# Sampling with source tiles of 9 by 14 for 3 by 8 positions, and hats of tile columns loaded into the weights' place

## Chip, cores, metric

One core of a Trainium2 chip. The metric is the device time of one execution in microseconds (us), the median of several; the fast runs of one kernel agree within 0.7% here, mostly within 0.4%, and all runs here were of the fast state. Engines: PE (TensorE, matmul), PEld (its weight loads), DVE (VectorE), ACT (ScalarE), POOL (GpSimd), SP (SyncE, which here only issues DMA).

## The reference, cut to what matters

Two layers on x of shape (2, 256, 128, 128). The first has three branches with dilations 1, 9 and 12. Each computes 18 offsets per pixel by a 3x3 convolution, samples x bilinearly at nine shifted places, weights the nine samples per channel and sums them.

```python
def _bilinear(x, py, px):            # four corners, each with weight (1-|py-yc|) * (1-|px-xc|)
    ...
def _deform_dw(x, offset, w, pad, dil):
    py = yy[None, None] - pad + ky[None, :, None, None] * dil + off[:, :, 0]
    px = xx[None, None] - pad + kx[None, :, None, None] * dil + off[:, :, 1]
    sampled = _bilinear(x, py, px)
    return jnp.einsum('bckhw,ck->bchw', sampled, wk)
# ... layer norm, gelu, sum of branches, 1x1 convolution, MLP, layer norm; then a ternary 3x3 convolution
```

The kernel turns sampling into matmuls. A tile of source pixels (8 rows by 16 columns, 128, with their channels) is the stationary operand. The moving operand A holds for each source pixel and each sampled position its bilinear weight: a *row hat*, max(0, 1-|dy|), times a *column hat*. Hats are computed first and kept in HBM; a unit of work (image, row block, branch) loads them for its tile rows and columns.

## The kernel before

The parts that the change touches, with `# ...` at cuts:

```python
RI, CI = 2, 10                                  # positions of a tile: 2 rows by 10 columns
TR, TC = RI + 2 * REACH, CI + 2 * REACH         # source pixels of a tile: 8 by 16 = 128 partitions

def load_hats(u):                               # issued on SP, a unit ahead
    for ky in taps(u):
        hy = pool.tile([P, RI, 3, W], F32, name="hy", tag="hy", bufs=3)
        hx = pool.tile([P, RI, 3, W], F32, name="hx", tag="hx", bufs=3)
        for h, first, dims in ((hy, 0, [[0, TC], [pitch, TR]]), (hx, TR, [[pitch, TC], [0, TR]])):
            nc.sync.dma_start(h[:, i0:i1]..., bass.AP(hq[first, y0]..., dims + [[1, (i1 - i0) * 3 * W]]))

def build(u, ky):                               # DVE: A = hy * hx, each tap shifted by its dilation
    pin(nc.vector.tensor_tensor(dst, hy[...], hx[...], ALU.mult))

def sample(u, c):                               # c: half of the channels
    tail.advance()                              # a slice of norm, gelu, MLP of rows that are done
    for T in range(0, NT, 2):
        # ... two matmuls of one source tile each (L759), then one copy PSUM -> ev (L768)
    if c == KC - 1:
        prepare(u + 2)                          # the products of unit u+2, then load_hats(u+3)
    for ky in kys:
        accumulate(u, c, ev, ky)                # DVE: ring += weight * ev, nine taps (L733)
```

`ev` holds sampled values, `ring` the rows of sums of a branch, and the tail is what is done with finished rows: norm, gelu, 1x1 convolution, MLP. The tail's own loads (`other`, `xn`, `xr`) are also issued on SP.

## Time and profile before

| | before |
|---|---|
| time | 7899 us (7881 to 7907) |
| first norm, offsets, hats | 0 to 981 us |
| sampling and tail | 981 to 6670 us |
| second convolution | 6670 to 7903 us |

The prediction below shows the lines that carry this. Only the sampling stage matters. Its slices of granted PE clock and DMA share, in tenths, over 40 equal parts of the span of the kernel before:

```profile
PEclk9999889999999999999999999999999999799999
DMA  8767799999999999998689999999999995222121
```

The clock is at nine tenths or more nearly throughout, and the DMA engines are 90% busy or more in nearly all of the stage.

### The profile page before, as it was taken

What the parts mean: (1) busy time and instruction counts of PE and PEld (TensorE: products, weight loads), DVE (VectorE), ACT (ScalarE), POOL (GpSimd) and SP (SyncE); (2) the same over time, 40 slices, a digit from 0 to 9 for tenths busy, and PEclk for the clock granted to TensorE, in tenths of its full rate; (3) what the DMA queues carried; (4) which work ended last, traced back from release to release, by engine and by line L of the source; (5) the groups of instructions that cost most, each with busy time, mean ns of one, the idle gap of its engine ahead of it and who ended that gap; (6) DMA issues with size and microseconds to landing.
All of it is one profiled execution on the core that took longest, in us unless ns stands there. A gap on an engine that the chain in (4) does not pass through costs nothing. (4 is left out here: it accounts for less than half of the span.)

```text
span 7903.1 us, 115440 instructions
## 1 busy us (share of the span) xinstructions
PE 7101.1 (90%) x37984; PEld 5421.9 (69%) x37984; DVE 6400.1 (81%) x13680; ACT 4514.7 (57%) x9350; POOL 715.1 (9%) x1292
## 2 busy tenths in 40 slices
PE   5999887899999999899988989999998999699999
PEld 2555577777887777777777777877787777344444
DVE  6666578888999889988688898898889986577776
ACT  1344355666666666667655666666666666333232
POOL 0000000111111111111100111111111111000000
PEclk9999889999999999999999999999999999799999
DMA  8767799999999999998689999999999995222121
GB/s 280 215 187 195 187 229 243 235 247 246 244 240 249 242 243 241 246 243 224 192 233 243 239 248 245 243 240 245 249 240 244 243 242 162 74 74 78 63 82 48
DMA packets 1011327, 1652.66 MB, mean 209 GB/s; under 512 B 120800, under 2 KB 573200, under 8 KB 1006360
## 3 DMA queue, kind: packets, MB, share of 16 engines
q1 hardware_dynamic: 993304, 1611.57, 76.3%
q10 hardware_dynamic: 17408, 33.56, 1.3%
q8 instruction: 304, 4.98, 0.3%
q14 instruction: 311, 2.55, 0.1%
HBM read 1376.69 MB, written 268.09 MB: 208 GB/s over the span
## 5 line engine op out<-in xcount | busy, mean ns | idle before, releaser
L759 PE MATMUL pm<-A,xs 128*128 128x180 f32 (+2 forms) x22288 | 3638.8, 319 | 578.6 <-ACT ev L768 551.2
L759 PEld LDWEIGHTS pm<-A,xs 128*128 128x128 f32 x22288 | 3431.7, 196 | 791.6 <-ACT ev L768 652.0
L768 ACT COPY ev<-pm 128x360 f32<-128x360 f32 (+2 forms) x5572 | 2283.3, 456 | 1517.3 <-DVE ring L733 751.3
L733 DVE SCALAR_TENSOR_TENSOR ring<-ev,defw,ring 128x256 f32<-128x256 f32 (+5 forms) x6272 | 2786.9, 463 | 212.5 <-ACT ev L768 43.2
L689 DVE TENSOR_TENSOR A<-hy,hx 128x768 f32<-128x768 f32 x1130 | 1018.7, 946 | 343.5 <-DMA hx<-hats 170.7
L487 ACT ACTIVATE T<-T,rs 128x256 f32<-128x256 f32 x1280 | 663.8, 595 | 3.3 <-POOL rs L483 3.2
L1083 PE MATMUL pc<-cring,signs 128*128 128x512 bf16 x2304 | 522.8, 386 | 56.1 <-DVE signs L971 23.6
L480 POOL TENSOR_SCALAR rs<-mv 128x4 f32<-128x4 f32 x320 | 108.0, 337 | 5108.0 <-DVE mv L478 4133.9
L1083 PE MATMUL pc<-cring,sums 128*128 128x512 bf16 x2304 | 510.3, 380 | 0.0
L446 PE MATMUL hp<-T,w 128*128 128x512 f32 x1024 | 490.7, 604 | 7.8 <-ACT T L565 7.8
L476 DVE BATCH_NORM_STATS2 st<-T 128x6 f32<-128x256 f32 x1280 | 446.9, 412 | 23.2 <-ACT T L468 23.2
L203 PE MATMUL pz<-wz,xa 128*128 128x486 f32 x1024 | 461.2, 584 | 4.3 <-DVE zr L210 4.3
L1083 PEld LDWEIGHTS <-signs 128*128 128x128 bf16 x2304 | 227.5, 99 | 340.7 <-issue 46.2
L446 PE MATMUL h<-hT,w 128*128 128x512 f32 x1024 | 460.1, 592 | 0.0
L1083 PEld LDWEIGHTS <-sums 128*128 128x128 bf16 x2304 | 225.4, 98 | 274.4 <-DVE sums L1143 0.2
L499 PEld LDWEIGHTS zc<-ident,T 128*128 128x128 f32 x2560 | 342.0, 156 | 98.2 <-issue 61.5
L515 ACT ACTIVATE T<-zc,bb,bw 128x512 f32<-128x512 f32 x384 | 278.5, 779 | 227.8 <-PE zc L499 226.8
L499 PE MATMUL zc<-ident,T 128*128 128x128 f32 x2560 | 384.5, 297 | 19.6 <-ACT T L487 14.1
L1067 ACT CAST cring<-D 128x2048 bf16<-128x2048 f32 x128 | 243.3, 1902 | 222.9 <-PE pc L1083 152.2
L482 POOL TENSOR_TENSOR rs<-rs,mhalf 128x4 f32<-128x4 f32 x320 | 369.6, 1155 | 0.0
L468 ACT COPY T<-tp 128x512 f32<-128x512 f32 x640 | 345.2, 599 | 38.0 <-PE tp L466 37.3
L1091 ACT ACTIVATE o<-xl,l1b 128x1024 f32<-128x1024 f32 x64 | 73.5, 1149 | 506.9 <-DMA out_x<-o 431.7
(120 smaller groups left out, 5768.7 us busy)
## 6 DMA issues: line engine op xcount, KB each, us to landing
hy<-hats SPq DMA_DIRECT2D x1114, 384.0 KB, 6.4
hx<-hats SPq DMA_DIRECT2D x1114, 384.0 KB, 7.3
xs<-table SPq DMA_DIRECT2D x1876, 128.0 KB, 4.4
g12d<-T SPq DMA_DIRECT2D x128, 512.0 KB, 7.1
other<-g12d SPq DMA_DIRECT2D x128, 512.0 KB, 10.1
hats<-hb SPq DMA_DIRECT2D x192, 240.0 KB, 4.3
hats<-hb SPq DMA_DIRECT2D x192, 192.0 KB, 3.3
xl<-x1d SPq DMA_DIRECT2D x56, 640.0 KB, 4.1
```

Source lines behind the costliest of these rows:

```text
L203: nc.tensor.matmul(pz[:, 0:NZ], lhsT=xt[:, c, r, :], rhs=k["wz"][:, c, :], start=c == 0, stop=c == KC - 1,)
L446: nc.tensor.matmul(out, lhsT=w, rhs=v, start=i == 0, stop=i == n - 1)
L468: nc.scalar.copy(Tv[:, 2 * h : 2 * h + 2, :].rearrange("p j c -> p (j c)"), tp)
L476: pin(nc.vector.bn_stats(st[:, j, :], Tv[:, j, :]))
L482: nc.gpsimd.tensor_tensor(rs[:, 0, :], rs[:, 0, :], mhalf[:, 0:NB4], ALU.pow)
L487: nc.scalar.activation(Tv[:, j, :], Tv[:, j, :], AF.Identity, scale=rs[:, 0, j : j + 1], bias=rs[:, 1, j : j + 1],)
L499: nc.tensor.transpose(zc[:, j * P : (j + 1) * P], Tv[:, j, c * P : (c + 1) * P], ident)
L689: nc.vector.tensor_tensor(dst, hy[:, i0:i1].rearrange("p i t w -> p t i w"), hx[:, i0:i1].rearrange("p i t w -> p t i w"), ALU.mult,)
L733: nc.vector.scalar_tensor_tensor(dst, src, w, dst, ALU.mult, ALU.add)
L759: nc.tensor.matmul(pm[:, j, 0:n], lhsT=xts[b, Rt][T + j][:, c * P : (c + 1) * P], rhs=A[:, m0:m1, AO + (T + j) * CI : AO + (T + j + 1) * C ...
L768: nc.scalar.copy(ev[:, m0:m1, T * CI : (T + 2) * CI].rearrange("p m (t j) -> p t m j", j=CI), pm[:, :, 0:n].rearrange("p t (m j) -> p t m ...
L1083: nc.tensor.matmul(pc[:, bank, :], lhsT=w[:, m * P : (m + 1) * P], rhs=xc[:, i, k, t * JC : (t + 1) * JC, kx : kx + W], start=j == 0, stop ...
```

## The change

The intent: fewer, longer instructions on DVE, which paces the stage, and no buffers for column hats. The diff, cut to its core:

```diff
-RI, CI = 2, 10
+RI, CI = 3, 8
-RINGS = (12, 28, 32)
+RINGS = (8, 28, 32)
+HBUFS = 2
+SLOTS = 3
-LAG = 5
+LAG = 6
@@ hats
+        def load_columns(u):
+            for ky in taps(u):
+                src, at, n = hat_rows(u, ky, TR, [[HY * 3 * W, TC], [0, TR]])
+                nc.sync.dma_start(k["A"][u % 2][0:PT, AO + at : AO + at + n], src)
+        def load_rows(u, ky):
+            hy = pool.tile([P, RI * 3 * W], F32, name="hy", tag="hy", bufs=HBUFS)
+            nc.sync.dma_start(hy[0:PT, 0:n], src)
+            hys.append((hy, u, at, n))
+        def build():
+            hy, u, at, n = hys.popleft()
+            A = k["A"][u % 2][0:PT, AO + at : AO + at + n]
+            pin(nc.vector.tensor_tensor(A, A, hy[0:PT, 0:n], ALU.mult))
+            following = next(ahead, None)
+            if following:
+                load_rows(*following)
@@ sample
+                    rhs = bass.AP(A.tensor,                       # the taps' shift, on read
+                        A.offset + AO + q0 * 3 * W + dil + (T + j) * CI - REACH,
+                        [[A.ap[0][0], PT], [3 * W, q1 - q0], [W - dil, 3], [1, CI]])
 ...
-            if c == KC - 1:
-                prepare(u + 2)
-            for ky in kys:
-                accumulate(u, c, ev, ky)
+            if last:
+                load_columns(u + 2)
+            due = len(taps(u + 2)) if last else 0
+            for i, ky in enumerate(kys):
+                accumulate(u, c, sums, ky)
+                if i and due:
+                    build()
+                    due -= 1
+            for _ in range(due):
+                build()
```

A tile now has 9 by 14 source pixels, 126 partitions. Of the hat loads of 128 partitions most often 16 packets are in flight at once (1792 us of the span before), of those of 126 most often 14, which the texts below call 16 and 14 engines. The 1x1 convolution also gets its norm's scale on ScalarE instead of in the weights, which frees a copy of them.

More of the change, by code (lines that the diff above doesn't have):

```diff
@@ L45 @@
 WT = NT * CI + 2 * REACH
-AO = 12
-WA = 28 + W
-NH = TR + TC
+PT = TR * TC
+AO = 16 + REACH
+AE = 13
+NH = 24
 HALF = 64
-RINGS = (12, 28, 32)
+RINGS = (8, 28, 32)
 BRS = (0, 1, 2)
@@ L53 @@
 VBUFS = 9
+HBUFS = 2
 PEAK = 3
 GAP = 2
-LAG = 5
-XCLS = (0, 1, 2, 8, 9)
+SLOTS = 3
+LAG = 6
+XCLS = (0, 1, 4, 7)
 NPAT = RI + len(XCLS) + 1
@@ L94, in conv_preact_kernel @@
     gmask = load("gmask", [P, P], t["gmask"])
-    convs = [
-        load(f"convw{b}", [P, KC, C], t["convw"].rearrange("(k p) o -> p k o", p=P))
-        for b in range(NB)
-    ]
-    negmean = [const.tile([P, KC], F32, name=f"negmean{b}") for b in range(NB)]
+    convw = load("convw", [P, KC, C], t["convw"].rearrange("(k p) o -> p k o", p=P))
+    shifts = [const.tile([P, KC], F32, name=f"shift{b}") for b in range(NB)]
     w1 = load("w1", [P, KC, HID], t["w1"].rearrange("(k p) o -> p k o", p=P))
@@ L120, in conv_preact_kernel @@
     HY = H + 3
-    hats = dram("hats", [NOFF // 6, TR + TC, HY, 3, W])
+    hats = dram("hats", [NOFF // 6, NH, HY, 3, W])
     offd = dram("offd", [H, W, NOFF])
@@ L291, in make_hats @@
                 nc.tensor.transpose(pp[0:HALF, 1, cols], parts[:, 1, r0 + r, 0:HALF], ident_b)
-            pl = k["planes"][g % 2]
+            pl = k["planes"][g % RI]
             nc.vector.tensor_copy(pl[:, 0, :], pp[:, 0, :])
@@ L344, in conv_preact_kernel @@
             "zr": ap.tile([P, ZRING, NZ], F32, name="zr"),
-            "planes": [ap.tile([P, 2, NG], BF16, name=f"planes{i}") for i in range(2)],
+            "planes": [ap.tile([P, 2, NG], BF16, name=f"planes{i}") for i in range(RI)],
         }
@@ L352, in conv_preact_kernel @@
         nc.vector.tensor_copy(k["hatw"], hatw)
-        pattern = ap.tile([P, NG], F32, name="pattern")
-        nc.sync.dma_start(pattern[HALF : HALF + NPAT], t["pattern"])
-        for pl in k["planes"]:
-            nc.vector.tensor_copy(
-                pl[HALF : HALF + NPAT, 1, :], pattern[HALF : HALF + NPAT]
-            )
+        for v, pl in enumerate(k["planes"]):
+            pattern = ap.tile([P, NG], F32, name="pattern", tag="pattern", bufs=1)
+            nc.sync.dma_start(pattern[HALF : HALF + NPAT], t["pattern"][v])
+            nc.vector.tensor_copy(pl[HALF : HALF + NPAT, 1, :], pattern[HALF : HALF + NPAT])
         for parts in k["parts"]:
@@ L376, in conv_preact_kernel @@
             gn1.append((mean, rstd))
-            nc.vector.tensor_scalar(negmean[b], mean, -1.0, None, ALU.mult)
-            for c in range(KC):
-                nc.vector.tensor_scalar(
-                    convs[b][:, c, :], convs[b][:, c, :], rstd[:, c : c + 1], None, ALU.mult
-                )
+            nc.vector.scalar_tensor_tensor(shifts[b], mean, -1.0, rstd, ALU.mult, ALU.mult)
             phase_a(b, ap, psum, k)
@@ L538, in branch @@
                     nc.scalar.activation(
-                        xn[:, c, :], xn[:, c, :], AF.Identity, bias=negmean[b][:, c : c + 1]
+                        xn[:, c, :], xn[:, c, :], AF.Identity,
+                        scale=gn1[b][1][:, c : c + 1], bias=shifts[b][:, c : c + 1],
                     )
@@ L551, in finish @@
                 self.matmul(
-                    pc, [(convs[b][:, c, m * P : (m + 1) * P], xn[:, c, :]) for c in range(KC)]
+                    pc, [(convw[:, c, m * P : (m + 1) * P], xn[:, c, :]) for c in range(KC)]
                 )
@@ L629, in sample_near @@
         units = [(b, Rt, br) for b in range(NB) for Rt in range(NR) for br in BRS]
-        xts, hbs, owners, begun = {}, {}, {}, set()
+        xts, hys, owners, begun = {}, deque(), {}, set()
         done = {(b, br): 0 for b in range(NB) for br in BRS}
@@ L636, in load_tiles @@
             for T in range(NT):
-                xt = pool.tile([P, C], F32, name="xs", tag="xs", bufs=20)
+                xt = pool.tile([P, C], F32, name="xs", tag="xs", bufs=NT + 5)
                 src = bass.AP(
@@ L642, in load_tiles @@
                 )
-                nc.sync.dma_start(xt, src)
+                nc.sync.dma_start(xt[0:PT], src)
                 xts[b, Rt].append(xt)
@@ L653, in taps, with hat_rows @@
             return [ky for ky in (-1, 0, 1) if valid(units[u][1], units[u][2], ky)]
-        def load_hats(u):
+        def hat_rows(u, ky, first, dims):
             b, Rt, br = units[u]
-            for ky in taps(u):
-                i0, i1 = valid(Rt, br, ky)
-                hq = hats[b][br * 3 + ky + 1]
-                y0 = Rt * RI - REACH - ky * DILS[br] + i0
-                hy = pool.tile([P, RI, 3, W], F32, name="hy", tag="hy", bufs=3)
-                hx = pool.tile([P, RI, 3, W], F32, name="hx", tag="hx", bufs=3)
-                pitch = HY * 3 * W
-                for h, first, dims in (
-                    (hy, 0, [[0, TC], [pitch, TR]]),
-                    (hx, TR, [[pitch, TC], [0, TR]]),
-                ):
-                    src = hq[first, y0]
-                    nc.sync.dma_start(
-                        h[:, i0:i1].rearrange("p i t w -> p (i t w)"),
-                        bass.AP(src.tensor, src.offset, dims + [[1, (i1 - i0) * 3 * W]]),
-                    )
-                hbs[u, ky] = hy, hx
@@ L675, in build @@
-        def build(u, ky):
-            b, Rt, br = units[u]
-            dil = DILS[br]
-            i0, i1 = valid(Rt, br, ky)
-            hy, hx = hbs.pop((u, ky))
-            Af = k["A"][u % len(k["A"])].rearrange("p t i w -> p (t i w)")
-            dst = bass.AP(
-                Af.tensor,
-                Af.offset + ((ky + 1) * 3 * RI + i0) * WA + AO + REACH - dil,
-                [list(Af.ap[0]), [RI * WA + dil, 3], [WA, i1 - i0], [1, W]],
-            )
-            pin(
-                nc.vector.tensor_tensor(
-                    dst,
-                    hy[:, i0:i1].rearrange("p i t w -> p t i w"),
-                    hx[:, i0:i1].rearrange("p i t w -> p t i w"),
-                    ALU.mult,
-                )
-            )
+            i0, i1 = valid(Rt, br, ky)
@@ new lines, in hat_rows @@
+            src = hats[b][br * 3 + ky + 1, first, Rt * RI - REACH - ky * DILS[br] + i0]
+            at = ((ky + 1) * RI + i0) * 3 * W
+            n = (i1 - i0) * 3 * W
+            return bass.AP(src.tensor, src.offset, dims + [[1, n]]), at, n
+        def load_columns(u):
+            for ky in taps(u):
+                src, at, n = hat_rows(u, ky, TR, [[HY * 3 * W, TC], [0, TR]])
+                nc.sync.dma_start(k["A"][u % 2][0:PT, AO + at : AO + at + n], src)
+        def load_rows(u, ky):
+            src, at, n = hat_rows(u, ky, 0, [[0, TC], [HY * 3 * W, TR]])
+            hy = pool.tile([P, RI * 3 * W], F32, name="hy", tag="hy", bufs=HBUFS)
+            nc.sync.dma_start(hy[0:PT, 0:n], src)
+            hys.append((hy, u, at, n))
@@ L719, in accumulate @@
                     dst = ring[:, c, y % n_ring : y % n_ring + j - i, x0:x1]
-                    src = ev[:, tap * RI + i : tap * RI + j, u0 : u0 + x1 - x0]
+                    src = ev[:, ky + 1, i:j, kx + 1, u0 : u0 + x1 - x0]
                     if new:
@@ L741, in sample @@
             b, Rt, br = units[u]
+            dil = DILS[br]
             kys = taps(u)
-            tail.advance()
+            last = c == KC - 1 and u + 2 < len(units)
             if not kys:
-                tail.advance()
-                if c == KC - 1:
-                    prepare(u + 2)
+                for _ in range(SLOTS):
+                    tail.advance()
+                if last:
+                    load_columns(u + 2)
+                    for ky in taps(u + 2):
+                        build()
                 return
-            A = k["A"][u % len(k["A"])].rearrange("p t i w -> p (t i) w")
-            m0, m1 = (kys[0] + 1) * 3 * RI, (kys[-1] + 2) * 3 * RI
-            n = (m1 - m0) * CI
+            A = k["A"][u % 2]
+            q0, q1 = (kys[0] + 1) * RI, (kys[-1] + 2) * RI
+            n = (q1 - q0) * 3 * CI
             ev = pool.tile([P, 9 * RI, NT * CI], F32, name="ev", tag="ev", bufs=2)
             for T in range(0, NT, 2):
-                if T // 2 == NT // 4:
+                if T // 2 % (NT // 2 // SLOTS + 1) == 0:
                     tail.advance()
                 pm = psum.tile([P, 2, 256], F32, name="pm", tag="pm", bufs=4)
-                for j in range(2):
+                nt = min(2, NT - T)
+                for j in range(nt):
+                    rhs = bass.AP(
+                        A.tensor,
+                        A.offset + AO + q0 * 3 * W + dil + (T + j) * CI - REACH,
+                        [[A.ap[0][0], PT], [3 * W, q1 - q0], [W - dil, 3], [1, CI]],
+                    )
                     pin(
@@ L760, in sample @@
                             pm[:, j, 0:n],
-                            lhsT=xts[b, Rt][T + j][:, c * P : (c + 1) * P],
-                            rhs=A[:, m0:m1, AO + (T + j) * CI : AO + (T + j + 1) * CI],
+                            lhsT=xts[b, Rt][T + j][0:PT, c * P : (c + 1) * P],
+                            rhs=rhs,
                             start=True,
@@ L768, in sample @@
                     nc.scalar.copy(
-                        ev[:, m0:m1, T * CI : (T + 2) * CI].rearrange(
+                        ev[:, q0 * 3 : q1 * 3, T * CI : (T + nt) * CI].rearrange(
                             "p m (t j) -> p t m j", j=CI
                         ),
-                        pm[:, :, 0:n].rearrange("p t (m j) -> p t m j", j=CI),
+                        pm[:, 0:nt, 0:n].rearrange("p t (m j) -> p t m j", j=CI),
                     )
                 )
-            if c == KC - 1:
-                prepare(u + 2)
-            for ky in kys:
-                accumulate(u, c, ev, ky)
-        def prepare(u):
-            if u < len(units):
-                for ky in taps(u):
-                    build(u, ky)
-                if u + 1 < len(units):
-                    load_hats(u + 1)
-        load_tiles(*units[0][0:2])
-        load_hats(0)
-        prepare(0)
-        prepare(1)
+            if last:
+                load_columns(u + 2)
+            due = len(taps(u + 2)) if last else 0
+            sums = ev.rearrange("p (q i t) x -> p q i t x", q=3, t=3)
+            for i, ky in enumerate(kys):
[4 more added lines that the diff above has]
+            for _ in range(due):
+                build()
+        load_tiles(*units[0][0:2])
+        ahead = iter([(u, ky) for u in range(len(units)) for ky in taps(u)])
+        for _ in range(HBUFS):
+            load_rows(*next(ahead))
+        for u in range(2):
+            load_columns(u)
+            for ky in taps(u):
+                build()
         for u, (b, Rt, br) in enumerate(units):
@@ L910, in conv_preact_kernel @@
             k = {
-                "A": [pool.tile([P, 9, RI, WA], F32, name=f"A{i}") for i in range(2)],
+                "A": [pool.tile([P, AO + 9 * RI * W + AE], F32, name=f"A{i}") for i in range(2)],
             }
@@ L1190 @@
     shift = np.stack([px[:, None] == px[None, :] + dx for dx in dxs], 1).astype(np.float32)
-    pattern = np.ones((NPAT, R, W), np.float32)
-    for m in range(RI):
-        pattern[m] = ((np.arange(R) + REACH + m) % RI)[:, None]
+    pattern = np.ones((RI, NPAT, R, W), np.float32)
+    for v in range(RI):
+        for m in range(RI):
+            pattern[v, m] = ((v * R + np.arange(R) + REACH + m) % RI)[:, None]
     for i, m in enumerate(XCLS):
-        pattern[RI + i] = ((np.arange(W) + REACH + m) % CI)[None, :]
+        pattern[:, RI + i] = (np.arange(W) + REACH + m) % CI
     hatw = np.zeros((P, 2, NTAP * NH), np.float32)
@@ L1217 @@
         "shift": shift,
-        "pattern": pattern.reshape(-1, NG),
+        "pattern": pattern.reshape(RI, NPAT, NG),
         "hatw": hatw,
```

## The prediction

> **What bounds the kernel now.** I read the source view of the sampling matmul first, because it dates the stage that the change touches, then the table of stretches, then the waits inside a steady stretch, then the groups by form.
>
> ```profile
> L759 PE MATMUL pm<-A,xs x22288: 216/315/669, 980.6 to 6669.6; 128*128 128x180 f32 x171, 128*128 128x120 f32 x24, 128*128 128x60 f32 x4
> 2000.00:3000.00 1000.00, 910.81 (x5132) 788.06 (x5133) 898.27 (x2050) 681.07 (x1468) 131.61 (x228) 0.97 0.93 243
> 7000.00:7903.00 903.00, 876.12 (x4023) 394.42 (x4020) 633.78 (x717) 262.51 (x160) 0.74 (x1) 0.99 0.19 68
> ```
>
> Sampling runs from 981 to 6670 us: 5690 of 7903 us. What comes before (norm, offsets, hats) and after (second convolution) keeps its instructions, so the whole difference must come from these 5690 us. The columns of the stretches are length, busy PE, weight loads, DVE, ACT, POOL, clock, DMA share, GB/s. In a steady 1000 us PE shows 911, DVE 898 and DMA 0.93: no engine has much room, and busy time alone doesn't say which one sets the pace. The waits of the same 1000 us do:
>
> ```profile
> ACT ev L768 <- DVE ring L733: 123.0, 64, 4.0
> PE pm L759 <- ACT ev L768: 89.4, 47, 3.6
> DVE A L689 <- PE pm L759: 25.6, 10, 2.6
> DVE ring L729 <- ACT ev L768: 19.9, 16, 1.7
> DVE A L689 <- DMA hx<-hats: 12.1, 15, 1.9
> DVE T L593 <- PE h L446: 10.0, 11, 1.1
> ```
>
> PE waits for evictions (89 us), evictions wait for DVE to finish with one of the two ev buffers (123 us), while DVE waits for everything together only some 70 us. So **DVE paces the stage**, with PE close behind. DMA is busy, but what waits for it is 12 us.
>
> PE is less full than it looks, as ends of matmuls are modelled. A run without waits gives the real pitch:
>
> ```profile
> 5024.09 4.43 PE L759 MATMUL pm<-A,xs 128*128 128x180 f32 x28
> ```
>
> 4.43 us less the last one's 0.33, over 27, is 152 ns for 180 columns: 0.84 ns a column, and each source matmul stands twice. The durations that I scale, and the loads:
>
> ```profile
> L768 ACT COPY ev<-pm 128x360 f32<-128x360 f32 x4788 | 2037.6, 472 | 1320.7 <-DVE ring L733 688.0 <-PE pm L759 388.8 <-PE hp L446 12.5
> L768 ACT COPY ev<-pm 128x240 f32<-128x240 f32 x672 | 220.6, 374 | 140.9 <-DVE ring L733 63.4 <-PE pm L759 43.1 <-issue 13.5
> L733 DVE SCALAR_TENSOR_TENSOR ring<-ev,defw,ring 128x256 f32<-128x256 f32 x2832 | 1366.7, 483 | 110.3 <-ACT ev L768 43.2
> L733 DVE SCALAR_TENSOR_TENSOR ring<-ev,defw,ring 128x128 f32<-128x128 f32 x360 | 104.3, 344 | 0.7
> L689 DVE TENSOR_TENSOR A<-hy,hx 128x768 f32<-128x768 f32 x1114 | 1011.1, 951 | 339.3 <-DMA hx<-hats 170.3 <-PE pm L759 143.0 <-DMA other<-g12d 15.4
> hx<-hats SPq DMA_DIRECT2D x1114, 384.0 KB, 7.3
> xl<-x1d SPq DMA_DIRECT2D x56, 640.0 KB, 4.1
> ```
>
> [...] 243 GB/s at share 0.93 is 261 GB/s at full share while sampling, 68 at 0.19 is 358 in the last stage. [...]
>
> **The change part by part.** A unit (row block, branch) was 2 rows and is 3; units go from 402 to 264. Counts of instructions are from the two built programs.
> - PE: 11,144 matmuls of mostly 180 columns become 8,976 of mostly 216. Columns fall from 1,898,400 to 1,840,896; times 2 times 0.84 ns that is 97 us less.
> - DVE, weighted sums (L733): 7060 instructions with the first writes become 5052 on nearly the same elements. 483 to 344 ns for 256 to 128 elements is 1.09 ns an element; I use 1.04 and a fixed 216 ns. The new forms then take 616 (384 elements), 597 (366) and 588 (357). Before: 2832x483 + 1448x473 + 1376x467 + small ones = 2906 us; after: 1616x616 + 904x597 + 912x588 + small ones = 2502. First writes: 267 to 223.
> - DVE, building A: 1130 products of 768 become 752 of mostly 1152[...]: 1068 to 1013 us. Together DVE loses 404+44+55, about 500 us counted singly, and since its neighbours overlap a little in the trace (busy 2787, not 2906) I take **400 us**.
> - ACT: 5572 evictions become 4752. 472 to 374 ns for 120 elements is 0.82 ns an element, so 531 ns for 432: 2348 us against 2283. Slightly more, on an engine at 68%: off the path.
> - DMA: hats 882 to 866 MB, tiles 246 to 193 MB, the tail's 234 MB as they are.
> - What it moves: column hats are loaded straight into A, so not before PE has finished the unit two earlier; before, they went to buffers of their own. And row hats have two buffers for three products, so the third load of a unit can't start before the first product is done.
>
> The new wait, per unit: from the end of the first product to the third, DVE has three sums (3x0.6) and a product (1.36): 3.15 us. The load takes 0.5 to issue and some 4 to land, by the 4.1 us of the 640 KB load in the uncrowded last stage: 4.5. That leaves **1.4 us of DVE idle per unit**. The columns land about 4.5 us after PE ends the unit; DVE then has the last eviction (1.2) and six sums (3.5) to go, so that wait is about zero.
>
> Pace: before, 102 products in 500 us are 34 units, 14.7 us each, or 22.4 us for three rows. DVE is busy 0.898x14.7 = 13.2, times 402/264 is 20.1, less 400/264 = 1.5 is 18.6. To it come the row wait 1.4, the waits for evictions and tail that stay (33 of 1000 us, 0.7) and gaps between instructions (0.6): **21.3 us**. PE's own floor: sampling 34x2x216x0.84 = 12.3; the tail's matmuls 1643 us over 264 = 6.2 (their columns at the same pitch); over a clock of 0.97 that is 19.1, plus small gaps, so PE stays just under DVE. 21.3/22.4 of 5690 is 5411: about 280 us less, or 7620. I shade it to **7640**, since two nearly equal engines lose some to each other.
>
> **The rivals.**
> (a) The in-place chain becomes the bound: PE ends a unit, columns land, products, the next unit but one. For it: DVE runs in program order, so a late load stops sums that are ready. If loads take 7 us, as hats do now, the third product waits 4 us: 23.9 us a unit, 5690x23.9/22.4 = 6070, or 8280 in all. Against: the DMA engines should be less crowded.
> (b) Fourteen engines saturate. If a byte costs an engine what it does now (261/16 = 16.3 GB/s), the busiest carry (866+193)/14 + 234/16 = 90.3 MB, 5540 us of DMA at least: 7750, and loads stay late. Against: [...] packets get faster and the mean DMA share falls to about 0.65.
> (c) The row wait is swallowed, because other waits shrink by it: 19.9 us, 5055 us, 7270 in all. For it: DVE was the engine that others waited for. Against: PE's floor of 19.1 with some 10% of waits is 21.
>
> **Range and chances.** Between (c), which PE's floor cuts to about 7400, and (b) with some of (a), about 7860. The central sum is 3.3% faster, and a stall of 1 us more per unit takes 260 us of it away; a gain below 2% is thus quite possible, a loss over 2% needs (a) in full. Faster 0.68, same 0.27, slower 0.05.
>
> **What would show each step.** The stage should still start near 981 us and last about 5430. L733's successor should show 615 ns for 384 elements, the product 1350 ns, the eviction of 432 about 530. In a steady stretch the products' waits should name the load of hy, about 1.4 us per unit, and PE rather than DVE should be the fuller engine. [...] 0.85 or more (14 of 16) says that (b) holds. I am wrong if products wait over 3 us per unit, if matmuls with runs of 8 columns take a longer pitch than 0.84 ns a column, or if the eviction grows well beyond 530 ns.

## The result, and the profile after

8450 us (8443 to 8463) against 7890 us on the same chip: ratio 1.071, 95% interval 1.068 to 1.074. Ratios here are the mean time of one kernel's runs over that of the other's runs of the same rounds, so not quite the ratio of the medians quoted. The change is 7% slower, where 3% faster was predicted.

The source view of the sampling matmul and the stretch that was shown of before, now of the changed kernel (columns as in the prediction):

```profile
L753 PE MATMUL pm<-A,xs x17952: 227/344/730, 957.6 to 7198.3; 126*128 126x216 f32 x174, 126*128 126x144 f32 x21, 126*128 126x72 f32 x5
```

```profile
2000.00:3000.00 1000.00, 837.76 (x3976) 698.00 (x3975) 746.25 (x1453) 585.02 (x1193) 108.26 (x204) 0.92 0.68 208
```

The stage lasts 6240 us instead of 5690, so it carries all of the loss. In the steady stretch DVE fell from 898 to 746, PE from 911 to 838, the DMA share from 0.93 to 0.68 and the clock from 0.97 to 0.92: everything is emptier. That is what waiting looks like, and not what a full engine looks like. The slices of the whole span agree:

```profile
PEclk9999789999999999999989898999999999899999
DMA  8777667666666766666667666766666666311121
```

The instructions themselves cost what was expected. Groups by form, with count, busy time and the mean of one in ns:

```profile
L762 ACT COPY ev<-pm 128x432 f32<-128x432 f32 x3680 | 1778.9, 526 | 1625.6 <-DVE ring L716 894.0 <-PE pm L753 624.5 <-issue 61.1
L675 DVE TENSOR_TENSOR A<-A,hy 126x1152 f32<-126x1152 f32 x736 | 996.4, 1355 | 1095.1 <-DMA hy<-hats 557.7 <-DMA A<-hats 458.8 <-PE pm L753 76.8
L716 DVE SCALAR_TENSOR_TENSOR ring<-ev,defw,ring 128x384 f32<-128x384 f32 x1616 | 994.7, 616 | 34.9 <-ACT ev L762 2.1
L712 DVE TENSOR_SCALAR ring<-ev,defw 128x384 f32<-128x384 f32 x444 | 265.5, 598 | 90.5 <-ACT ev L762 90.4
```

Only the first writes (L712) do not: 598 ns, where the 223 us of the prediction amount to 408. The waits of the steady 1000 us, of the changed kernel (us in total, how often, the longest):

```profile
ACT ev L762 <- DVE ring L716: 146.0, 36, 8.4
...
ACT xn L531 <- DMA xn<-in_x: 89.2, 10, 15.1
DVE A L675 <- DMA A<-hats: 82.9, 22, 7.2
DVE A L675 <- DMA hy<-hats: 76.6, 40, 3.2
...
PE pc L439 <- ACT xn L531: 56.2, 10, 14.2
DVE T L549 <- PE pc L439: 46.7, 20, 5.3
```

The stretch has 121 products, so 40.3 units of 24.8 us. Per unit, DVE is busy 18.5 us (predicted 18.6), waits 2.1 us for columns (0), 1.9 for rows (1.4), and 1.2 us for a matmul of the tail's 1x1 convolution, which waits for ACT, which waits for `xn`, loaded late. In the kernel before, ACT waited 4 us for `xn` in the whole stage; now 524 us. The load itself is unchanged; only `SLOTS` and `LAG` shift when the tail runs. Why it is late stands in SP's own part of the timeline. The columns are start, how long, what (a length of several issues includes SP's waits between them):

```profile
2421.22 2.45 SPq L663 DMA_DIRECT2D A<-hats  x3
2428.45 0.78 SPq L668 DMA_DIRECT2D hy<-hats  x1
2429.27 0.54 SPq L519 DMA_DIRECT2D other<-g12d  x1
2431.52 3.77 SPq L668 DMA_DIRECT2D hy<-hats  x2
2435.38 0.58 SPq L527 DMA_DIRECT2D xn<-in_x  x1
2438.98 11.41 SPq L637 DMA_DIRECT2D xs<-table  x12
2450.45 0.52 SPq L594 DMA_DIRECT2D xr<-in_x  x1
2451.07 0.80 SPq L637 DMA_DIRECT2D xs<-table  x1
2451.97 0.78 SPq L663 DMA_DIRECT2D A<-hats  x1
```

And DVE's products in the same stretch, with the idle time before them in brackets:

```profile
2427.06 1.36 DVE L675 TENSOR_TENSOR A<-A,hy 126x1152 f32<-126x1152 f32 x1 [1.16 <-DMA A<-hats]
2430.14 1.35 DVE L675 TENSOR_TENSOR A<-A,hy 126x1152 f32<-126x1152 f32 x1
2433.11 1.36 DVE L675 TENSOR_TENSOR A<-A,hy 126x1152 f32<-126x1152 f32 x1 [1.62 <-DMA hy<-hats]
```

Read the two together. The first product ends at 2428.42, and only then does SP issue the row load for the third (2428.45), which lands 4.7 us later: the predicted row wait. But SP issues in program order here. The next row load waits for the second product (ends 2431.49), the one after for the third (2434.47), and `xn`, whose last matmuls ended at 2368.5, is issued only behind them, at 2435.38. Next come 12 source tiles, in 11.4 us, and only behind those the next columns, at 2451.97. So each kind of load stands behind waits of the other kinds.

### The profile page after: what moved, and what is told of

It is laid out like the page before. It is cut to its first block, busy times and chain, and to the rows that moved or that the text cites. A ratio compares the mean times of both kernels' runs of the same rounds, so it can differ in the third digit from the quotient of the medians.

```text
span 8442.1 us, 100684 instructions
## 1 busy us (share of the span) xinstructions
PE 7101.1 (84%) x33648; PEld 5312.0 (63%) x33648; DVE 6038.2 (72%) x11291; ACT 4360.6 (52%) x8530; POOL 668.2 (8%) x1292
## 5 line engine op out<-in xcount | busy, mean ns | idle before, releaser
L753 PE MATMUL pm<-A,xs 126*128 126x216 f32 (+2 forms) x17952 | 3571.1, 353 | 757.0 <-ACT ev L762 625.7
L753 PEld LDWEIGHTS pm<-A,xs 126*128 126x128 f32 x17952 | 3273.9, 199 | 1048.1 <-ACT ev L762 738.0
L762 ACT COPY ev<-pm 128x432 f32<-128x432 f32 (+2 forms) x4752 | 2092.6, 490 | 1826.2 <-DVE ring L716 949.6
L716 DVE SCALAR_TENSOR_TENSOR ring<-ev,defw,ring 128x384 f32<-128x384 f32 (+6 forms) x4472 | 2393.5, 560 | 101.8 <-ACT ev L762 2.1
L675 DVE TENSOR_TENSOR A<-A,hy 126x1152 f32<-126x1152 f32 (+2 forms) x752 | 1010.0, 1344 | 1149.0 <-DMA hy<-hats 575.1
L439 PE MATMUL pc<-xn,convw 128*128 128x512 f32 x512 | 323.9, 791 | 358.3 <-ACT xn L531 337.5
L439 PEld LDWEIGHTS pc<-xn,convw 128*128 128x128 f32 x512 | 125.5, 257 | 522.2 <-ACT xn L531 395.7
L712 DVE TENSOR_SCALAR ring<-ev,defw 128x384 f32<-128x384 f32 (+2 forms) x580 | 301.9, 529 | 106.6 <-ACT ev L762 106.5
L531 ACT ACTIVATE xn<-xn,shift,gn_rstd 128x512 f32<-128x512 f32 x128 | 97.2, 806 | 538.1 <-DMA xn<-in_x 535.7
L461 ACT COPY T<-tp 128x512 f32<-128x512 f32 x640 | 344.9, 598 | 42.2 <-PE tp L459 40.3
L492 PE MATMUL zc<-ident,T 128*128 128x128 f32 x2560 | 348.8, 283 | 19.7 <-ACT T L480 9.3
```

Of the source, the lines that this page charges most:

```text
L439: nc.tensor.matmul(out, lhsT=w, rhs=v, start=i == 0, stop=i == n - 1)
L461: nc.scalar.copy(Tv[:, 2 * h : 2 * h + 2, :].rearrange("p j c -> p (j c)"), tp)
L492: nc.tensor.transpose(zc[:, j * P : (j + 1) * P], Tv[:, j, c * P : (c + 1) * P], ident)
L675: pin(nc.vector.tensor_tensor(A, A, hy[0:PT, 0:n], ALU.mult))
L716: nc.vector.scalar_tensor_tensor(dst, src, w, dst, ALU.mult, ALU.add)
L753: nc.tensor.matmul(pm[:, j, 0:n], lhsT=xts[b, Rt][T + j][0:PT, c * P : (c + 1) * P], rhs=rhs, start=True, stop=True,)
```

## The experiments

**The theory** after the result: the geometry saves what was predicted, and the way hats are loaded loses more, by loads that are asked for late and stand in each other's way on SP. **The rivals**: the geometry itself is slow (short runs, the longer unit, a lower clock), or loads of 126 rows, with 14 packets in flight rather than 16, can't deliver. Ratios are to the kernel before of the same rounds. The changed kernel's own times (8450 us) are from its own job; its kernel before there, 7890 us, is within 0.1% of those of the other jobs, so medians may be compared to a few tens of us.

**The loading alone, on the old tiles.**

```diff
-RI, CI = 3, 8            # and rings, column classes, SLOTS, LAG as before the change
+RI, CI = 2, 10
```

> The changed kernel with the tile sizes of the kernel before (2 rows by 10 positions, rings of 12 rows, two tail slots a sampling pass, as there), so the way of loading hats alone: columns straight into A, rows in two buffers. Theory (the loading scheme makes fixed waits per unit: columns about 2 us, rows about 2 us, and late tail loads about 2 us of 24.8): the same waits come back 402 times instead of 264, so clearly slower than the kernel before: 8700 to 9300 us. Rival (the geometry costs: runs of 8 columns, 14 DMA engines, a longer unit): within 3% of the kernel before, 7700 to 8100 us.

8851 us, ratio 1.121. With the tiles of before, the new loading alone costs 12%. DVE's waits in e1's stage:

```profile
DVE A L675 <- DMA hy<-hats: 939.4, 344, 9.7
DVE A L675 <- DMA A<-hats: 295.8, 148, 12.7
```

These two are 1235 us, where DVE waited 171 us for hats in the kernel before. So the loss is there without the geometry; whether the geometry adds to it, the next two runs show. (`xn` was not late in this run: PE waited 5 us for it. But e1 also has the old `SLOTS` and `LAG`, so whether these or the order of the loads spared it was not taken apart.)

**Neither loading nor its waits, for both geometries.**

```diff
-                nc.sync.dma_start(k["A"][u % 2][...], src)           # and no load of hy
-            pin(nc.vector.tensor_tensor(A, A, hy[0:PT, 0:n], ALU.mult))
+            pin(nc.vector.tensor_tensor(A, hc[1][0:PT, 0:n], hc[0][0:PT, 0:n], ALU.mult))   # constants
```

> The changed kernel without any load of hats: every product multiplies two constant tiles into A, all else as it is (wrong on purpose). Theory (the tiles of 3 by 8 do save DVE and PE work; what loses the time is the waits for hats and the tail loads held behind them): DVE at 18.6 us a unit and PE at some 19.5 set the pace, 20.5 to 21.5 us a unit instead of 24.8, so 7400 to 7650 us; xn's wait goes too, as SyncE no longer stops at row loads; clock back at 0.96 or more. Rival (the geometry itself is slow: runs of 8, the clock, the longer unit): over 8000 us.

> The kernel before with the same done to it: no load of hats, products of two constant tiles (wrong on purpose). Its DVE waited 186 us for hats and 147 for PE before products; without the first at most 150 us are to be had, so 7700 to 7880 us. With e5 this gives what the geometry is worth when no load is waited for: theory 150 to 400 us in favour of 3 by 8, rival nothing or a loss.

e5 took 7358 us (ratio 0.934; 42 us below its range), e6 7772 us (0.985). Their outputs are wrong, which doesn't matter for the times. So 3 by 8 is worth 413 us when no hat is waited for, and the rival of a slow geometry falls; the prediction had reckoned 400 us of DVE work. (Without hat loads the DMA share is only some 0.25 in both, so crowding is taken away along with the waits.) And loading hats costs the kernel before 116 us, the changed one 1091. The steady stretch of e5:

```profile
2000.00:3000.00 1000.00, 946.06 (x4757) 804.78 (x4755) 890.79 (x1722) 704.01 (x1434) 127.73 (x240) 0.98 0.25 80
```

It has 145 products: 20.7 us a unit, with PE at 946 the fullest engine and the clock back at 0.98. So the low clock of the changed kernel goes with its waits (0.92 with them, 0.98 without); how much of its time the low clock itself costs was not measured apart.

**One wait at a time.** Tail loads on ACT's queue:

```diff
-            nc.sync.dma_start(other, gv)
+            nc.scalar.dma_start(other, gv)                 # xn and xr likewise
```

> The changed kernel with the tail's three loads (other, xn, xr) issued from ScalarE's queue instead of SyncE's, where they stand behind loads of row hats that wait for products. Theory (the in-order SyncE queue holds them up): the waits ACT xn <- DMA (524 us), PE pc <- ACT xn (337) and DVE T <- PE pc (234) nearly vanish and the time falls by 200 to 350 us, to about 8180 us; the granted clock rises from 0.93. Rival (DMA is late whoever issues): the waits stay and the time is within 50 us of the changed kernel.

8283 us, ratio 1.050. DVE's wait for the 1x1 convolution fell from 234 to 25 us and ACT's for `xn` from 524 to 160: SP's order had held them up. But the gain is 166 us, less than the 200 to 350 expected, while row waits rose from 575 to 754 us.

Three row buffers (wrong, to make room):

```diff
-HBUFS = 2
+HBUFS = 3
```

> The changed kernel with three buffers for row hats instead of two. To make room the second MLP weight and the 1x1 convolution's weight share the first's memory and both images share one statistics tile, so the result is wrong on purpose; no instruction of the sampling changes otherwise. Theory (the third row load of a unit waits for the first product): DVE A <- DMA hy falls from 575 us to under 150 us, and the time by 150 to 400 us, to about 8200 us; the wait for columns (470 us) stays. Rival (the loads themselves are slow to land): the row wait falls by less than a third, time within 80 us of the changed kernel.

8328 us, ratio 1.055, 122 us less, short of the 150 to 400 expected. The row wait is gone from the list, and others took over. DVE's two longest in e3, columns and the 1x1 convolution:

```profile
DVE A L673 <- DMA A<-hats: 622.3, 225, 14.4
DVE T L547 <- PE pc L437: 414.7, 119, 10.7
```

They were 470 and 234 us in the changed kernel.

Columns in two buffers of their own (wrong: e3's sharing of memory, and three source tiles fewer in advance, where the expectation says two):

```diff
+            hx = pool.tile([P, RI * 3 * W], F32, name="hx", tag="hx", bufs=HBUFS)
+            nc.sync.dma_start(hx[0:PT, 0:n], src)
-            pin(nc.vector.tensor_tensor(A, A, hy[0:PT, 0:n], ALU.mult))
+            pin(nc.vector.tensor_tensor(A, hx[0:PT, 0:n], hy[0:PT, 0:n], ALU.mult))
```

> The changed geometry with the column hats loaded beside the row hats into two buffers of their own, and the product written to A, as the kernel before did (with two instead of three buffers each; two source tiles fewer in advance, and the memory sharing of the three-row-buffer run, so wrong on purpose). Theory (the in-place columns wait for PE): DVE A <- columns' load in A is gone, but every third product of a unit now waits for two loads issued behind one another, so of the 470 us for columns about half come back as waits for hx; time 8150 to 8400 us. Rival (in-place loading costs nothing, the row buffers everything): the sum of waits before products stays at 1050 to 1150 us and the time within 60 us of the changed kernel.

8399 us, ratio 1.064, almost no gain, and DVE waits 1385 us for hx alone, more than for rows and columns together before. So taking the columns out of A gains nothing as long as two buffers serve three products. That loading in place costs nothing is not shown: with three row buffers (e3) columns were the longest wait.

**Several together.** Tail on ACT and three row buffers, paid for by four source tiles fewer in advance:

```diff
-HBUFS = 2                                          # and tail loads on nc.scalar, as in e2
+HBUFS = 3
-                xt = pool.tile([P, C], F32, name="xs", tag="xs", bufs=NT + 5)
+                xt = pool.tile([P, C], F32, name="xs", tag="xs", bufs=NT + 1)
```

> A version meant to be correct: tail loads on ScalarE's queue and three row buffers, paid for by four source tiles fewer in advance. Theory (the waits fed each other, each alone being taken over by the others): rows' 575 us and xn's 234 us both go, the columns' grows to 500 to 700 us; 8000 to 8150 us. Rival (only columns count): 8200 us or more.

8109 us, ratio 1.029, correct. The two together gain 340 us, where 166 and 122 of each alone make 288; the surplus is about what comparing jobs leaves open. What is left is columns: 837 us, more than the 500 to 700 expected.

Source tiles on GpSimd's queue on top of that:

```diff
-                nc.sync.dma_start(xt[0:PT], src)
+                nc.gpsimd.dma_start(xt[0:PT], src)
```

> The same with the source tiles loaded from GpSimd's queue, so that SyncE has only hats and stores, and columns no longer stand behind 12 tile loads of 0.95 us each at every third unit. Theory: the columns' wait falls by a third to a half and the time to 7850 to 8050 us. Rival: GpSimd's own work (the power for the norms) is held up behind loads that wait for PE, ScalarE's normalising waits for it and the time is no better than with tiles on SyncE.

7951 us, ratio 1.008, correct. Columns still cost 671 us, a fifth less, where a third to a half was expected, and PE now waits 287 us for tiles. So most of the columns' wait was not due to tiles ahead of them on the queue.

**Products half a unit later**, to give the columns time to land:

```diff
+            following = taps(u + 1) if c == 0 and u + 1 < len(units) else []
-            due = len(taps(u + 2)) if last else 0
+            due = len(following)
-                if i and due:
+                if due:
```

> The changed kernel with one thing moved: the products for a unit are no longer made right after PE has left its A (in the sums of the second half of the unit two earlier), but half a unit later, one after each tap row's sums of the first half of the unit one earlier. Two row buffers, everything on SyncE's queue, in-place columns, all as changed. Theory (the loss is latency of loads that DVE asks for at once, not their throughput): columns have some 10 us to land and the third row load 5 us, so the waits for A and hy fall from 1045 us to under 250 us, the tail's loads no longer stand behind row loads (xn under 100 us), and the time is 7450 to 7700 us, clock 0.96. Rival (DMA can't deliver 3 by 8 in time, 14 engines of 16): the waits move to PE <- DVE A, time over 8000 us.

8355 us, ratio 1.058, correct: 95 us less than the changed kernel, but this expectation failed badly, by some 650 us. The column wait did fall, from 470 to 91 us, but rows kept 494 us in waits of up to 14 us, and now PE waits for the products. From e9's waits of PE and of SP:

```profile
PE pm L754 <- DVE A L675: 611.6, 109, 15.6
```

```profile
SPq L668 <- DVE ring L716: 2214.1, 454, 14.4
```

SP stood 2214 us before row loads until DVE got to the product that frees their buffer (the trace names the sums beside it); the same line was 1451 us in the changed kernel's stage. So a later product keeps the row loads' buffers, and SP with them, waiting longer. Latency alone was not the cause.

Products ahead of the sums, and e9 with the tail on ACT:

> The same with each product ahead of its tap row's sums instead of after them, so that PE gets A sooner and DVE waits sooner. If PE now waits for A in e9, this is faster than e9; if waits for loads are still what is left, it is slower by 20 to 150 us.

> e9 with the tail's loads on ScalarE's queue. If e9 has already freed SyncE's queue, nothing is left to gain: within 40 us of e9. If xn still waits there over 200 us, it is 50 to 150 us faster than e9.

e10 took 8196 us (1.037): faster than e9, so PE's wait for A was the tighter end (612 to 497 us). Against the changed kernel the move thus gains 254 us in this order, with nothing else changed. e11 took 8273 us (1.048): 82 us gained, so SP's queue was not freed by e9 alone.

e9's order with the old tiles:

> e9 with the tile sizes of the kernel before (2 by 10). Theory: with latency hidden the new way of loading costs no more than the old one, so 7800 to 8000 us, and e9 beats it by what the geometry is worth, some 300 to 450 us as between e5 and e6. Rival (in-place loading costs something however it is timed): over 8100 us.

8903 us, ratio 1.128. The expectation failed as e9's did: with the old tiles the later product gains nothing (e1 took 8851 us). Rows still kept 626 us here.

**Everything out of each other's way.** e13 is e10 with three row buffers, the tail on ACT and four tiles fewer in advance; e14 adds all source tiles on GpSimd's queue; e15 only every second one:

```diff
-                nc.sync.dma_start(xt[0:PT], src)
+                (nc.gpsimd if T % 2 else nc.sync).dma_start(xt[0:PT], src)      # e15
```

> Products half a unit later and ahead of the sums (e10), with three row buffers and the tail's loads on ScalarE's queue; the source tiles still on SyncE's queue, four fewer in advance. If late row loads were what e10 still lost (488 us of DVE, 497 of PE waiting for its products), 7750 to 7950 us. If the queue is still stopped by tile loads that wait for PE, over 8000 us with waits of SyncE for PE before tile loads and late columns.

> e13 with the source tiles loaded from GpSimd's queue, so that only hats and stores stand on SyncE's. Theory (a, the order on one queue): waits for A and hy together under 200 us, PE waits for tiles some 290 us as in e8; 7550 to 7800 us, faster than the kernel before. Rival (b, throughput): DMA share over 0.85 or row and column waits over 500 us, and not faster than e8's 7950 us.

> e13 with every second source tile on GpSimd's queue and the others on SyncE's. If GpSimd's pace of issue is what makes PE wait for tiles in e8, that wait falls from 290 us to under 100 us and this is faster than e14 by up to 150 us; if SyncE's order is what counts, it lies between e13 and e14.

| | time, us | ratio to before | DVE waits for columns | PE waits for tiles | PE waits for products |
|---|---|---|---|---|---|
| e13 | 7980 | 1.011 | 264 | 77 | 373 |
| e14 | 7922 | 1.003 | 149 | 302 | 36 |
| e15 | **7643** | **0.970** (0.967 to 0.973) | 158 | 72 | 162 |

All three are correct, and row waits are gone from all. e13 missed its range by 30 us, and e14 its 7550 to 7800 by 122. In e14 one queue issues all 17 tiles of a row block:

```profile
L637 POOL DMA_DIRECT2D xs<-table x1496: 592/592/942, 940.9 to 6631.1; - x187
```

That is 592 ns for each load, while PE takes a tile in 0.39 us (12 records, six tiles, in 2.36 us from 2423.62 in the changed kernel), so PE waits. SP is no faster an issuer (786 ns in e15), but two queues together are. e15 gained 279 us on e14, more than the 150 expected, and PE's wait for tiles fell from 302 to 72 us, as its reading said. Whether GpSimd's own norm work on the same queue added to that wait was not taken apart. **e15 beats both kernels**: 3.0% faster than the one before. Its steady stretch:

```profile
2000.00:3000.00 1000.00, 922.28 (x4596) 785.39 (x4596) 865.28 (x1680) 686.04 (x1388) 210.91 (x356) 0.97 0.79 242
```

It moves 242 GB/s at a share of 0.79, so loads of mostly 126 rows deliver what this pace needs. The rival of throughput falls as the cause of the loss. (e15 still takes 285 us more than e5, which loads no hats.)

**Is it the geometry or the queues?** e16 is e15 with the products back where the change has them; e17 is the kernel before with e15's two changes of queue.

> e15 with the products back where the change has them (three row buffers, tail on ScalarE's queue, every second tile on GpSimd's). If columns asked for too late are a cause of their own, DVE waits 500 to 800 us for columns again, as in e7 and e8, and it takes 7850 to 8000 us. If the queues were the whole cause, within 80 us of e15.

> The kernel before with the tail's loads on ScalarE's queue and every second source tile on GpSimd's, nothing else. Its SyncE queue held up little (DVE waited 171 us for hats, PE 2 us for tiles), so 7780 to 7920 us: e15's gain is then the geometry's. If it falls to 7700 or below, e15's gain is mostly the queues'.

e16: 7835 us, ratio 0.993, correct; DVE waits 574 us for columns, against 158 in e15. It lies 15 us under its range and 190 us above e15: columns asked for too late are a cause of their own. e17: 7935 us, ratio 1.006, 15 us above its range. The kernel before gains nothing from these two queues. That e15's 3% needs the geometry is not fully shown, as e15's whole way of loading on the old tiles was not run; but e15 is also 129 us faster than e6, the kernel before without any hat load.

Tried but not run: three row buffers in the changed kernel as it is, for which the build asks 195.9 KB per partition with 192.1 left, hence the sharing of memory in e3; loading two source tiles with one DMA did not build.

## Why the prediction was wrong

- **The stage, and who paces it.** The stage is right: the start (958 us against 981) and the last stage (1244 us against 1233) hardly moved. That DVE rather than PE paces it was argued from the waits and not tested; without hat loads (e5) PE is the fuller of the two, 946 against 891.
- **Work per instruction.** Right but for one term. Predicted and measured: sums of 384 elements 616 and 616 ns, products 1350 and 1355, evictions of 432 elements 531 and 526, DVE busy per unit 18.6 and 18.5 us. What the product would take could be read from the trace before: 553 ns for 384 elements and 951 for 768 make an estimate of 1349 for 1152. All products were reckoned at 1013 us and took 1010. The 1.04 ns an element and the fixed 216 for sums were an estimate; 344 ns for 128 elements and 616 for 384, measured after, are 1.06 an element. The new matmuls keep the pitch of 0.84 ns a column (12 records in 2.36 us from 2423.62, the last one some 0.35), so the rival of short runs falls too. One comparison was of unlike things: 2348 us of evictions is count times mean, 2283 us is busy time with overlaps counted once. By busy time they fell from 2283 to 2093 us. The first writes were mis-sized: reckoned 223 us in all, measured 302. In the trace before they take 276 ns for 128 elements and 342 for 256, which makes an estimate of 408 for 384; after the change three rows of 128 take 598 ns, while two still take 340. Why is not shown; no run takes it apart.
- **DMA share.** Predicted 0.65, measured 0.68, with 126-row loads; the rival of saturation, (b), did not happen. That the numbers are so close is luck: the loads were spread over a slower pace than predicted. At the predicted pace, in e15, the share is 0.79, nearer to the 0.85 that was to confirm (b). That packets get faster is shown: a packet of hats took 198 ns for 3072 bytes before and 242 ns for 4608 after, so 15.5 and 19.0 GB/s. That this would bring the share to 0.65 was the author's estimate: the 261 and 358 GB/s that the prediction sets side by side come from different loads.
- **The row wait.** Right in kind: 1.4 us predicted, 1.9 measured. The issue of one load takes 0.78 us, not 0.5; this load landed 4.7 us after its issue began, not 4.5, and a load of columns 5.8.
- **"The columns land about 4.5 us after PE ends the unit ... so that wait is about zero."** Wrong: 2.1 us. With the rows' 1.9 the products waited 4.0 us a unit, above the 3 that the prediction named as its sign of being wrong. This step, and the next, failed in part from the same assumption: that a load is issued when its own wait is over. Columns were issued behind up to 13 source tiles; in the same stretch of 1000 us, SP waited for PE before columns only some 40 us in 121 loads, so it was mostly SP that came late. Once issued at 2421.22, the first of three landed 5.8 us later, so the time to land was short by more than a microsecond as well. Late issue behind tiles is the smaller part by the later runs: all tiles off the queue took 166 of 837 us from the columns' wait (e7, e8), a later product 416 of 574 (e16, e15).
- **"The waits for evictions and tail that stay (33 of 1000 us, 0.7)."** Wrong: 1.8 us per unit. A wait that the prediction doesn't know came: `xn` behind row loads, 524 us of ACT and 337 of PE in the stage. SP's order made most of it: with these loads on ACT's queue ACT's wait was 160 us (e2), and without hat loads, at the same `SLOTS` and `LAG`, it was below 28 (e5).
- **The sum.** 18.6 and 21.3 us per unit were predicted for work and pace; 18.5 and 24.8 were measured. Of the 3.5 us between the two paces, 2.1 are columns, 0.5 rows and 1.1 the tail, less 0.2 us of smaller gaps.
- **PE's floor at a clock of 0.97.** It was 0.92 in the stretch. A wait of PE of up to 14 us, as in the tail's line above, wasn't in the sum. Over the runs the clock goes with the waits: 0.92 here, 0.97 in e15, 0.98 without hat loads (e5). What lowers it is not shown.
- **The rivals.** (a), the late load that stops DVE, was the right one, with 8280 us for waits of 4 us (the product of 2427.06 came 1.16 us late, and behind it three sums whose values were in `ev` since 2421.6); its waits came by a way I had not looked at. What I set against it, emptier DMA engines, was true (0.68) and did not help: part of the time went before issue, and a load still took 4.7 to 5.8 us to land in the stretch shown.
- **That a gain was there to be had.** e15 runs at 21.3 us a unit (141 products in 1000 us), the predicted pace, and in 7643 us. That it meets the predicted 7640 so closely is partly chance, as its waits are others than those predicted.

Open: how the changed kernel's own loss divides between late issue and late landing for columns, and how much of it the low clock adds, as each wait taken away alone was partly made good by another.

## What to carry to other kernels

Count a load's latency from when its *queue* gets to it, not from when its own condition holds: on a queue that issues in program order, as SP's did here, one load that waits for a product holds up every load behind it, also those of unrelated work (ACT's 524 us for `xn`, 160 with those loads on another queue). When buffers are cut so that loads become just-in-time, look at what else stands on that queue, and put loads that wait for different engines on different queues. Give such a load enough lead as well: making the products half a unit later gained 254 us on the changed kernel (e10) and 190 us with the queues freed (e15 against e16). And if single fixes gain little each, run them together before dropping them: each of these alone stayed slower than the kernel before, and only all together were clearly faster.

## What else the runs show

- Where loads are late, it matters which engines issue them: moving every second tile load off SP's queue took the time from 7980 to 7643 us (e13, e15). In the kernel before, where DVE waited 171 us for hats and PE 2 us for tiles, it gained nothing (e17, 1.006).
- The issue of a 126-row load takes 785 ns on SP, and 589 with 128 rows and the same code (e1); for source tiles, whose rows are equally long in both, it is 788 (changed kernel) and 548 (before). Why is not shown. The source views of the changed kernel and of e1:

```profile
L663 SPq DMA_DIRECT2D A<-hats x752: 779/785/2608, 951.0 to 7166.0; - x188
```

```profile
L663 SPq DMA_DIRECT2D A<-hats x1130: 514/589/2667, 963.2 to 7575.8; - x189
```

- Loads of 126 rows take a smaller share of the DMA engines: 243 GB/s took 0.93 with 128-row loads (before), 242 GB/s took 0.79 with mostly 126 rows (e15). The cause is open: packets are longer there too, 4608 bytes of hats against 3072.
- GpSimd issues such loads in 592 ns each (e14), where SP takes 786 (e15). With all 17 tiles of a row block on its queue PE waited 302 us for them (e14), with half of them 72 us (e15).
